# Counting with the mask as the moving operand: four mask tiles at once in quarters of the array

## Chip, cores and metric

The kernel runs on one core of one Trainium2 chip. The metric is the device time of one execution in microseconds (us); the profile shows one execution, with the busy time of each engine: PE (TensorE matmul), PEld (TensorE weight load, beside PE), DVE (VectorE), ACT (ScalarE), POOL (GpSimd) and SP (SyncE, which only issues DMAs here).

## The reference, cut to what matters

Four graph layers work on `x` (2708 x 512) with one dense adjacency matrix `adj` (2708 x 2708, float32, entries not negative, most of them zero). The change touches only the first:

```python
mask = incidence_m > 0
head = mask.astype(incidence_m.dtype)
head = head / jnp.maximum(jnp.sqrt(jnp.sum(head * head, axis=-1, keepdims=True)), EPS)
inc = incidence_m + head
edge_fea = inc @ cur
edge_degree = jnp.sum(inc, axis=-1, keepdims=True)
return edge_fea / edge_degree
```

So before a row of the matrix can be used, its positive entries must be counted: each positive entry is raised by one over the square root of the count of its row. The result goes through a residual and a layer norm, and layers 1 to 3 follow (sums over neighbours with gates and attention, three hops, a normalised convolution).

## The kernel before

The matrix lies transposed in memory (`adjT`: rows are neighbours, columns are the nodes whose sums are made). Nodes and neighbours are cut in two halves of 1354; a half has ten tiles of 128 and one of 74. A **sweep** passes once over the matrix for one layer. It goes through four **ranges** of columns, `RANGES0 = [(768, 256), (0, 384), (384, 384), (1024, 330)]` for the first sweep, each number pair a start and a width within a half. The first range is done plainly: eight products, ten steps each of 256 columns (line 469). The other ranges use a Strassen-like scheme with seven products (line 460: `accu`, `accc`, `accd`, `acca` are its PSUM accumulators; `T1` to `T4` are sums of feature tiles, `a` and `s` tiles of the matrix or sums of them made by DVE on line 405). A step is one tile of 128 neighbours for two column blocks of features; each float32 matmul shows as two passes in the trace, so a step is four passes.

Order is written as a list: `at(pos, fn)` puts a piece of work at a position (a product is one unit, a range seven units, the plain range eight), the list is sorted, and a scheduler then places the instructions on the engines, each of which works in order. Tiles come from pools with a fixed number of buffers: `ring` (38 tiles of the matrix and temporaries), `tmp` (17, among them the tiles loaded for counting), `mask` (6, bfloat16), PSUM (8 banks). A tile of a pool can be written only once the earlier user of its buffer is done.

The counts of a range are made while the range before it is in its products (`extra0`). For each half h of the columns and each of the 22 neighbour tiles i:

- `count_load` brings the tile of `adjT` into a `tmp` buffer, called `cl`. SP issues it for the first counted range, POOL for the later ones. The 74-row tiles need two DMAs.
- `count_mask` makes the mask by two ACT activations, Sign and Relu (lines 714 and 715).
- `count_tile` multiplies with ones: the mask is the stationary operand, 128 columns of it at a time, and a column of ones moves, so three matmuls of one column per tile add up to `cnt`, a PSUM tile with the counts of 128 nodes in each of three columns (line 725).

After the last tile `count_row` makes one over the square root of the count, with a refinement step (DVE, ACT and DVE again on `r`, lines 737 to 745), and `spread_row` lays it out along the free axis: three PE transposes into `pr` (line 753), an ACT copy to `row` (line 756). Then `prep0` (lines 771 and 772, DVE) raises the matrix tiles of the range. The first range's own counts come from the matrix tiles that it has loaded anyway; the same functions serve it.

The list puts the load of tile i 0.7 units ahead of its count, and the mask 0.35 units ahead. The 22 counts of a half are spread over 2.1 to 2.5 units. ACT also copies accumulators out (lines 514 and 531) and applies layer norms (line 567, waiting for DVE's line 564, which waits for the power on POOL, line 562). `run_sums` (lines 774 to 785) makes the row sums for `edge_degree` by matmuls with a column of ones, `rs`; `ds` on line 988 is the like in the second sweep.

The second sweep has a form that the change uses too (`gates` and `gate_tile`, lines 1008 to 1022): four matmuls with 32 stationary columns each, writing partitions 0, 32, 64 and 96 on of one PSUM bank `pg`, an ACT copy to `zg`, and a matmul with `pick` that adds the four partitions. `pick` has ones at rows 0, 32, 64 and 96 of its first column and at rows 1, 33, 65 and 97 of its second.

Of the kernel before, what the change touches and what calls it, by code (L numbers as in the profile page):

```python
# [25 lines left out]
P = 128  # L26
# [32 lines left out]
def wt(k):  # L59
    return min(P, NH - k * P) if k < KT else P  # L60
# [8 lines left out]
def gnn_kernel(ctx: ExitStack, tc: tile.TileContext, x, adjT, w_sa, a_sa, w_gcn, b_gcn, wab, bab, w_hop, w_out,  # L69
               b_out, out):  # L70
    nc = tc.nc
    N, D = x.shape
    NT = 2 * KT
# [13 lines left out]
    ones_bf = const.tile([P, P], BF, name="ones_bf")  # L87
# [27 lines left out]
    pick = const.tile([P, 2], F32, name="pick")  # L115
# [45 lines left out]
    def trans(nm):  # L161
        return pool.tile([P, 384], F32, name=nm, tag="ring", bufs=RING)
# [7 lines left out]
    def bank(nm, shape=None):  # L170
        return psum.tile(shape or [P, D], F32, name=nm, tag="x", bufs=8)
# [6 lines left out]
    def at(pos, fn, hold=False):  # L178

        def go():  # L180
            n = len(nc.cur_bb.bb.instructions)
            fn()
            held.update(range(n, len(nc.cur_bb.bb.instructions)))

        events.append((pos, len(events), go if hold else fn))
# [503 lines left out]
    cnt = {}  # L689
    V = {}  # L690

    def tiles_of(R0, n):
        return list(range(R0 // P, (R0 + n + P - 1) // P))

    def count_load(R0, n, h, i):
        w = wt(i % KT)
        t = tmp("cl")
        j0 = (i // KT) * NH + (i % KT) * P

        move(nc.sync if R0 == RANGES0[1][0] else nc.gpsimd, t[:w, :n], adjT[j0 : j0 + w, h * NH + R0 : h * NH + R0 + n])  # L700
        cnt[R0, h, i] = t

    def count_rows(R0, i):

        return {KT - 1: KA, NT - 1: 32}.get(i, P) if R0 == RANGES0[0][0] else wt(i % KT)

    def count_mask(R0, n, h, i, t=None, on_vector=False):
        w = count_rows(R0, i)
        t = cnt.pop((R0, h, i)) if t is None else t
        cnt[R0, h, i] = m = mask_tile()  # L710
        if on_vector:
            nc.vector.tensor_scalar(m[:w, :n], t[:w, :n], 0.0, None, ALU.is_gt)
        else:
            nc.scalar.activation(m[:w, :n], t[:w, :n], AF.Sign)
            nc.scalar.activation(m[:w, :n], m[:w, :n], AF.Relu)

    def count_tile(R0, n, h, i):

        w = count_rows(R0, i)
        m = cnt.pop((R0, h, i))  # L720
        if i == 0:
            cnt[h] = bank("cnt", [P, 4])
        for j, q in enumerate(tiles_of(R0, n)):
            wq = wt(q)
            nc.tensor.matmul(cnt[h][:wq, j : j + 1], m[:w, q * P - R0 : q * P - R0 + wq], ones_bf[:w, 0:1],
                             start=i == 0 and j == 0, stop=i == NT - 1, skip_group_check=True)

    def count_row(R0, n, h):


        ts = tiles_of(R0, n)
        r = small.tile([P, 4, 4], F32, name="r", bufs=2)
        ps = cnt.pop(h)
        if wt(ts[-1]) < P:
            nc.vector.memset(r[:, 0, :], 1.0)
        for j, q in enumerate(ts):
            nc.vector.tensor_scalar(r[: wt(q), 0, j : j + 1], ps[: wt(q), j : j + 1], 1.0, None, ALU.max)
        m = len(ts)

        c, y, q, t = (r[:, i, :m] for i in range(4))  # L740
        nc.scalar.activation(q, c, AF.Sqrt)
        nc.vector.reciprocal(q, q)
        nc.vector.tensor_tensor(t, q, q, ALU.mult)
        nc.vector.scalar_tensor_tensor(t, c, -0.5, t, ALU.mult, ALU.mult)
        nc.vector.scalar_tensor_tensor(y, t, 1.5, q, ALU.add, ALU.mult)
        cnt[R0, h] = r

    def spread_row(R0, n, h):
        r = cnt.pop((R0, h))
        pr = bank("pr")  # L750
        for j, q in enumerate(tiles_of(R0, n)):
            w = wt(q)
            nc.tensor.transpose(pr[:, q * P - R0 : q * P - R0 + w], r[:w, 1, j : j + 1].to_broadcast([w, P]),
                                ident[:w, :w])
        row[R0, h] = tmp("row")
        nc.scalar.copy(row[R0, h][:, :n], pr[:, :n])  # L756

    def add_run(R0, h, n, w, t):
        if (R0, h) not in run:
            run[R0, h] = tmp("run")  # L760
            if (R0, 1) in run and h == 0:

                nc.vector.tensor_tensor(run[R0, 0][:, :n], run[R0, 1][:, :n], t[:, :n], ALU.add)
                return
            nc.vector.tensor_copy(run[R0, h][:, :n], t[:, :n])
        else:
            nc.vector.tensor_tensor(run[R0, h][:w, :n], run[R0, h][:w, :n], t[:w, :n], ALU.add)
# [6 lines left out]
    def run_sums(R0, n, h, after):  # L774

        ps = bank("rs", [P, 4])
        t = run.pop((R0, h))
        ts = list(range(R0 // P, (R0 + n + P - 1) // P))
        for i, k in enumerate(ts):
            nc.tensor.matmul(ps[: wt(k), i : i + 1], t[:, k * P - R0 : k * P - R0 + wt(k)], ones_f, start=True,  # L780
                             stop=True)
        r = small.tile([P, 4], F32, name="rd", bufs=4)
        for i, k in enumerate(ts):
            after(r[: wt(k), i : i + 1], ps[: wt(k), i : i + 1], h * KT + k, wt(k))
            rd[h * KT + k] = r[:, i : i + 1]

    def extra0(pb, r, R0, n, A):
        if r == 0:
            for h, p, d in ((0, -3.7, 0.05), (1, 1.9, 0.055)):
                for j, i in enumerate([*range(KW), *range(KT, KT + KW), KT - 1, NT - 1]):  # L790
                    key = (f"{h + 1}{i // KT + 1}", i % KT) if i % KT < KW else ("r" if i < KT else "r32", h)
                    a = lambda key=key: A[(0,) + key]
                    at(pb + p + d * (j - 2 * h), lambda h=h, i=i, a=a: count_mask(R0, n, h, i, a(), h == 0 or i % KT == KT - 1))
                    at(pb + p + d * j, lambda h=h, i=i: count_tile(R0, n, h, i))
                    at(pb + (1.7 if h == 0 else 4.8) + 0.06 * j,
                       lambda h=h, i=i, a=a: add_run(R0, h, n, count_rows(R0, i), a()))
                at(pb + p + d * 22, lambda h=h: count_row(R0, n, h))
                at(pb + p + d * 22 + 0.1 * h, lambda h=h: spread_row(R0, n, h))
        if r + 1 < len(RANGES0):
            R1, n1 = RANGES0[r + 1]  # L800
            for h, p, d in ((0, 1.0, 2.5), (1, 3.8, 2.5)) if r else ((0, 3.2, 2.2), (1, 5.4, 2.1)):
                for i in range(NT):
                    q = pb + p + d * i / NT
                    at(q - 0.7, lambda i=i, h=h: count_load(R1, n1, h, i))
                    at(q - 0.35, lambda i=i, h=h: count_mask(R1, n1, h, i))
                    at(q, lambda i=i, h=h: count_tile(R1, n1, h, i))
                at(pb + p + d, lambda h=h: count_row(R1, n1, h))
                at(pb + p + d + 0.15, lambda h=h: spread_row(R1, n1, h))

        def inverse(o, s, t, w):  # L810
            nc.vector.reciprocal(o, s)

        at(pb + (5.2 if r else 3.3), lambda: run_sums(R0, n, 0, inverse))
        at(pb + (4.7 if r else 6.4), lambda: run_sums(R0, n, 1, inverse))
# [43 lines left out]
    for k in range(KW):  # L858
# [6 lines left out]
        at(7.5 + f, lambda k=k: x_last(k))  # L865
    at(9.3, start0)
    sweep(S[0], RANGES0, prep=prep0, extra=extra0, done=done0, first=True, sums=True)


# [79 lines left out]
    i = 0  # L949
# [624 lines left out]
    for n, i in enumerate(list(nc.cur_bb.bb.instructions)):  # L1574
        p = last if n < 3 * strict else done if n in held else {}
# [44 lines left out]
```

## Time and profile before

| | |
|---|---|
| three runs | 2884.59, 2882.81 and 2885.3 us, median 2884.59 |
| span of the profiled execution | 2884.5 us; no time around it is given apart |
| PE busy | 2836.5 us, 98% of the span |
| DVE busy | 2270.4 us, 79% |
| ACT busy | 569.2 us, 20% of the span, nearly all within the first 340 us when masks are made |
| POOL busy | 618.6 us, 21% |
| count matmuls, line 725 | 484, of 0.163 us each (median) |
| mask activations, lines 714 and 715 | 152 each; 0.507 us each (median) for 384 columns |

Busy is the time in which an engine has an instruction under way. Matmuls are pipelined, so the time between two starts, not the length of one, is what an instruction takes from PE. PEclk is the clock that was granted to PE, as a share of the full one. In a list of waits the engine on the left stood idle until the one on the right was done.

### The profile page before, as it was taken

What the parts mean: (1) busy time and instruction counts of PE and PEld (TensorE: products, weight loads), DVE (VectorE), ACT (ScalarE), POOL (GpSimd) and SP (SyncE); (2) the same over time, 40 slices, a digit from 0 to 9 for tenths busy, and PEclk for the clock granted to TensorE, in tenths of its full rate; (3) what the DMA queues carried; (4) which work ended last, traced back from release to release, by engine and by line L of the source; (5) the groups of instructions that cost most, each with busy time, mean ns of one, the idle gap of its engine ahead of it and who ended that gap; (6) DMA issues with size and microseconds to landing.
All of it is one profiled execution on the core that took longest, in us unless ns stands there. A gap on an engine that the chain in (4) does not pass through costs nothing. (4 is left out here: it accounts for less than half of the span.)

```text
span 2884.5 us, 37727 instructions
## 1 busy us (share of the span) xinstructions
PE 2836.5 (98%) x10963; PEld 1870.9 (65%) x10963; DVE 2270.4 (79%) x5879; ACT 569.2 (20%) x1122; POOL 618.6 (21%) x1119
## 2 busy tenths in 40 slices
PE   7999999999999999999999999999999999999998
PEld 6655665657765656866666666666666666666665
DVE  6998698576748675775699787887878878799987
ACT  4554200111146554542100000000000100100001
POOL 0223223123420101132203133031330211501202
PEclk9999999999999999999999999999999999999999
DMA  7666466354544333565668767566675666764542
GB/s 232 201 200 187 131 205 213 123 178 143 183 142 136 117 118 99 154 193 162 193 205 237 212 192 245 172 198 205 189 249 169 181 197 182 225 174 145 176 142 91
DMA packets 373455, 511.52 MB, mean 177 GB/s; under 512 B 63722, under 2 KB 326628, under 8 KB 373248
## 3 DMA queue, kind: packets, MB, share of 16 engines
q1 hardware_dynamic: 307128, 372.01, 44.1%
q0 software_dynamic: 49536, 126.39, 12.7%
q10 hardware_dynamic: 16584, 10.71, 1.3%
q8 instruction: 87, 1.43, 0.2%
q14 instruction: 120, 0.98, 0.1%
HBM read 425.22 MB, written 83.67 MB: 176 GB/s over the span
## 5 line engine op out<-in xcount | busy, mean ns | idle before, releaser
L1231 DVE TENSOR_TENSOR z<-z 128x339 f32<-128x339 f32 (+1 forms) x966 | 453.9, 502 | 13.0 <-PE accu L1286 4.0
L1304 ACT COPY q<-accu 128x338 f32<-128x338 f32 (+1 forms) x84 | 34.6, 443 | 1002.0 <-PE accu L1286 1000.2
L562 POOL TENSOR_TENSOR rstd<-rstd,neg_half 128x1 f32<-128x1 f32 (+3 forms) x91 | 58.4, 642 | 763.9 <-DVE rstd L561 516.3
L1286 PE MATMUL accc<-s,t 128*128 128x338 f32 (+1 forms) x644 | 198.2, 450 | 0.0
L1286 PE MATMUL accu<-z,t 128*128 128x338 f32 (+1 forms) x644 | 194.0, 448 | 1.6 <-DVE z L1231 1.6
L1286 PE MATMUL accd<-z,t 128*128 128x338 f32 (+1 forms) x644 | 193.9, 448 | 0.6 <-DVE q L1368 0.6
L1286 PE MATMUL accc<-z,t 128*128 128x338 f32 (+1 forms) x644 | 193.5, 448 | 0.5 <-ACT q L1304 0.5
L1419 POOL DMA_DIRECT2D Y<-y x192 | 104.9, 553 | 363.0 <-DVE y L1414 331.7
L405 DVE TENSOR_TENSOR a<-a,a 128x384 f32<-128x384 f32 (+2 forms) x330 | 161.2, 509 | 11.5 <-PE accu L460 10.7
L1286 PEld LDWEIGHTS accc<-s,t 128*128 128x128 f32 x644 | 120.9, 190 | 64.1 <-issue 7.5
L1286 PEld LDWEIGHTS accc<-z,t 128*128 128x128 f32 x644 | 122.0, 190 | 61.6 <-issue 1.0
L1286 PEld LDWEIGHTS accu<-z,t 128*128 128x128 f32 x644 | 121.7, 190 | 61.9 <-DVE z L1231 2.1
L1286 PEld LDWEIGHTS accd<-z,t 128*128 128x128 f32 x644 | 121.9, 190 | 60.5 <-DVE q L1368 1.5
L1231 DVE TENSOR_TENSOR s<-z 128x338 f32<-128x338 f32 (+1 forms) x322 | 149.5, 502 | 12.4 <-PE accc L1286 8.4
L1310 DVE TENSOR_TENSOR q<-q,accd 128x338 f32<-128x338 f32 (+1 forms) x112 | 55.9, 499 | 115.0 <-PE accd L1286 115.0
L1083 ACT ACTIVATE e<-row,neg_s 128x384 f32<-128x384 f32 (+5 forms) x176 | 100.5, 571 | 78.2 <-DVE e L1085 18.3
L1085 DVE TENSOR_TENSOR e<-e,f 128x384 f32<-128x384 f32 (+5 forms) x176 | 87.0, 505 | 22.6 <-ACT f L1084 21.5
L1084 ACT ACTIVATE f<-row,neg_s 128x384 f32<-128x384 f32 (+5 forms) x176 | 100.0, 568 | 18.7 <-DVE a L1086 4.5
L974 DVE SCALAR_TENSOR_TENSOR deg<-a,deg 128x384 f32<-128x384 f32 (+2 forms) x152 | 75.1, 504 | 19.8 <-DMA a<-in_adjT 18.7
L1086 DVE SCALAR_TENSOR_TENSOR a<-a,e 128x384 f32<-128x384 f32 (+2 forms) x160 | 79.7, 506 | 5.4 <-DMA a<-in_adjT 3.5
L408 POOL DMA_DIRECT2D As<-a x120 | 64.8, 543 | 83.5 <-DVE a L405 79.7
L771 DVE SCALAR_TENSOR_TENSOR s<-a,row 128x384 f32<-128x384 f32 (+2 forms) x152 | 75.2, 507 | 6.0 <-ACT row L756 6.0
(692 smaller groups left out, 5961.5 us busy)
## 6 DMA issues: line engine op xcount, KB each, us to landing
z<-As SPq DMA_DIRECT2D x320, 169.5 KB
z<-As SPq DMA_DIRECT2D x320, 169.0 KB
a<-in_adjT SPq DMA_DIRECT2D x240, 192.0 KB
z<-in_adjT SPq DMA_DIRECT2D x240, 169.5 KB
z<-in_adjT SPq DMA_DIRECT2D x240, 169.0 KB
a<-in_adjT SPq DMA_DIRECT2D x120, 165.0 KB
a<-in_adjT SPq DMA_DIRECT2D x112, 128.0 KB
As<-a POOLq DMA_DIRECT2D x60, 192.0 KB, 4.3
```

What stands on the lines that cost most here:

```text
L405: nc.vector.tensor_tensor(A[r, dst, k][:, :n], A[r, a, k][:, :n], A[r, b, k][:, :n], op)
L408: nc.gpsimd.dma_start(out=SD[m][k * P : (k + 1) * P, R0 : R0 + n], in_=A[r, dst, k][:, :n])
L562: nc.gpsimd.tensor_tensor(rstd[:w, 1:2], rstd[:w, 0:1], neg_half[:w], ALU.pow)
L771: nc.vector.scalar_tensor_tensor(t[:w, :n], a[:w, :n], 0.0, row[R0, h][:w, :n], ALU.is_gt, ALU.mult)
L974: nc.vector.scalar_tensor_tensor(d[:w, :n], a[:w, :n], 0.0, d[:w, :n], ALU.not_equal, ALU.add)
L1083: nc.scalar.activation(e[:w, :n], row[R0, h][0][:w, :n], AF.Exp, bias=neg_s[:w, t : t + 1])
L1084: nc.scalar.activation(f[:w, :n], row[R0, h][1][:w, :n], AF.Exp, bias=neg_s01[:w, t : t + 1])
L1085: nc.vector.tensor_tensor(e[:w, :n], e[:w, :n], f[:w, :n], ALU.min)
L1086: nc.vector.scalar_tensor_tensor(a[:w, :n], a[:w, :n], 0.0, e[:w, :n], ALU.not_equal, ALU.mult)
L1231: nc.vector.tensor_tensor(d[:, :n], Z[x + (k,)][:, :n], Z[y + (k,)][:, :n], op)
L1286: nc.tensor.matmul(B[home][:, :n], stat(v, k), a[:, :n], start=bool(start and k == 0), stop=k == nk - 1, skip_group_check=True)
L1419: nc.gpsimd.dma_start(out=rows[:, :, f * P : (f + 1) * P], in_=o[32 * f : 32 * (f + 1), : m * P].rearrange("p (b d) -> p b d", d=P))
```

## The change

For the three later ranges the mask becomes the moving operand. `count_four` runs for every fourth tile (and the last): it multiplies the four masks collected so far with 32 columns of ones each, the g-th into partitions 32g to 32g + 31 of one PSUM bank, so that each uses another quarter of the array's columns. The five full groups and one of two add up in the same bank, now 384 columns wide. `count_sums` then copies the bank to a ring tile `zc` on ACT and adds one partition from each quarter by three matmuls with the first column of `pick`, into another bank, `cs`, which `count_row` reads as it read `cnt`. The counts of the first range stay as they were.

```diff
+    def count_four(R0, n, h, i):
+
+        if i % 4 < 3 and i < NT - 1:
+            return
+        i0 = i - i % 4
+        if i0 == 0:
+            cnt[h] = bank("cnt", [P, 384])
+        for g in range(i - i0 + 1):
+            w = count_rows(R0, i0 + g)
+            m = cnt.pop((R0, h, i0 + g))
+            nc.tensor.matmul(cnt[h][32 * g : 32 * g + 32, :n], ones_bf[:w, :32], m[:w, :n], start=i0 == 0,
+                             stop=i0 + g + 4 >= NT, skip_group_check=True)
+
+    def count_sums(R0, n, h):
+
+        z = trans("zc")
+        nc.scalar.copy(z[:, :n], cnt[h][:, :n])
+        cnt[h] = ps = bank("cs", [P, 4])
+        for j, q in enumerate(tiles_of(R0, n)):
+            wq = wt(q)
+            nc.tensor.matmul(ps[:wq, j : j + 1], z[:, q * P - R0 : q * P - R0 + wq], pick[:, 0:1], start=j == 0, stop=True,
+                             skip_group_check=True)
 
     def count_row(R0, n, h):
 
@@
                     at(q - 0.7, lambda i=i, h=h: count_load(R1, n1, h, i))
                     at(q - 0.35, lambda i=i, h=h: count_mask(R1, n1, h, i))
-                    at(q, lambda i=i, h=h: count_tile(R1, n1, h, i))
+                    at(q, lambda i=i, h=h: count_four(R1, n1, h, i))
+                at(pb + p + d, lambda h=h: count_sums(R1, n1, h))
                 at(pb + p + d, lambda h=h: count_row(R1, n1, h))
                 at(pb + p + d + 0.15, lambda h=h: spread_row(R1, n1, h))
```

## The prediction

> **What bounds the kernel now.** I read first the busy time by stretch (columns: stretch, PE, PEld, DVE, ACT, POOL busy us with instruction counts, granted clock, DMA share, GB/s). The counts of the later ranges run between 55 and 330 us.
>
> ```profile
> 0.00:60.00 60.00, 43.58 (x247) 34.48 (x248) 36.56 (x119) 22.17 (x58) 0.70 (x6) 1.00 0.78 232
> 60.00:120.00 60.00, 56.18 (x350) 44.16 (x349) 51.34 (x149) 39.78 (x89) 6.23 (x11) 0.94 0.69 215
> 120.00:230.00 110.00, 109.75 (x490) 64.55 (x489) 96.46 (x244) 53.30 (x117) 32.42 (x58) 1.00 0.62 193
> 230.00:340.00 110.00, 110.00 (x489) 65.04 (x488) 87.88 (x214) 43.50 (x92) 29.91 (x53) 1.00 0.53 157
> ```
>
> From 120 to 340 us PE is the bound: time on it is time of the kernel, as far as DVE (80 to 88% busy) keeps up. From 60 to 120 us PE, ACT and DVE are all near their limit and the clock was granted at 0.94. Next, PE in order of time (start, length, engine, line):
>
> ```profile
> 150.20 1.54 PE L460 MATMUL accd<-a,T1A 128*128 128x384 f32 x4
> 151.57 0.22 PE L725 MATMUL cnt<-ones_bf,mask 74*128 74x1 bf16 x3
> 151.65 1.54 PE L460 MATMUL accd<-a,T1A 128*128 128x384 f32 x4
> 153.03 0.22 PE L725 MATMUL cnt<-ones_bf,mask 128*128 128x1 bf16 x3
> ...
> 158.83 0.59 PE L725 MATMUL cnt<-ones_bf,mask 128*128 128x1 bf16 x18
> 159.29 0.89 PE L460 MATMUL accc<-a,T4A 128*128 128x384 f32 x2
> ...
> 161.30 2.74 PE L460 MATMUL accd<-a,T1D 128*128 128x384 f32 x8
> 163.88 1.45 PE L460 MATMUL accu<-a,T2A 128*128 128x384 f32 x4
> ```
>
> Eight plain f32 passes take 163.88 - 161.30 = 2.58 us, 0.3225 each. Four passes and one count tile (three one-column matmuls) repeat every 153.03 - 151.57 = 1.46 us; less 4 x 0.3225 = 1.29, **a count tile costs PE 0.16 us**. Last, who waits for whom, 36 to 120 us for PEld and 0 to 340 us for ACT and POOL (total us, times, longest):
>
> ```profile
> PEld L725 <- ACT mask L715: 4.1, 6, 2.4
> PEld pr L753 <- DVE r L745: 2.5, 2, 2.2
> ACT mask L714 <- PE cnt L725: 33.6, 35, 4.1
> POOL cl L151 <- ACT mask L714: 70.2, 30, 18.1
> ```
>
> In the first counted range PE waits for masks; later ACT is up to six masks ahead and waits for a mask buffer (35 times), which only a count releases. So the ring of six is full and is what protects PE.
>
> **What the Trainium skill says.** "TensorEngine Tiling (Array Packing)", Key Properties: different tiles of the array load weights and multiply in parallel, and changing the tiling mode drains the engine. The second sweep already has this shape in f32 (gate sums, line 1012), and agrees:
>
> ```profile
> 514.92 0.81 PE L460 MATMUL accd<-a,B22B 128*128 128x384 f32 x2
> 515.66 0.52 PE L1012 MATMUL pg<-C,wab_pad 128*32 128x384 f32 x2
> 515.67 0.52 PE L1012 MATMUL pg<-W,wab_pad 128*32 128x384 f32 x2
> 516.01 0.49 PE L1012 MATMUL pg<-C,wab_pad 128*32 128x384 f32 x2
> 516.02 0.49 PE L1012 MATMUL pg<-W,wab_pad 128*32 128x384 f32 x2
> 516.45 1.56 PE L460 MATMUL accd<-a,B22B 128*128 128x384 f32 x4
> ```
>
> The quarters start about 10 ns apart. From 514.92 the two passes before should end at 515.565; the group holds PE from there to 516.45 = 0.885 us, and the first pass after it starts its successor about 0.10 late (the four passes take 1.40 instead of 1.29 us in the same pattern at 547.75): 0.98 in all, 0.34 more than its two streaming passes of 0.3225. That 0.34 is the drain into and out of quarter mode. "TensorE: Matmul & The Clock Gate", section "Wait — 56ns, not 53.3ns?", prices a warm matmul at N / 2.4 GHz + 2.5 ns: an estimated 0.16 us for 384 bf16 columns and 0.14 for 330. No run here shows a wide bf16 matmul; the f32 pass at 0.3225 is twice that, which fits. The same page, "What's actually happening", says that an idle window of about 3.4 us halves the clock for the next; the 0.94 above is two such windows, each costing 3.4 / 2 = 1.7 us.
>
> **The change, part by part.** (1) Removed: 3 ranges x 2 halves x 22 tiles = 132 count tiles. The 88 of 384 columns at 0.162 are 14.3, less 0.4 because six of them stand together (0.54 for 18 matmuls instead of 0.97); the 44 of 330 columns at 0.173 (same subtraction at 245 to 278 us) are 7.6. Sum **-21.5**. (2) Added: per range and half five groups of four and one of two, 36 in all. A group costs 0.34 + 0.16 = 0.50 (24 of them, 12.0) or 0.34 + 0.14 = 0.48 (12, 5.8): **+17.8**. A group of two pays the same. Bounds: 0.33 if half of the drain belongs to f32 weights, 0.66 if the stream runs at the f32 rate. (3) Added: the sums, six times three f32 matmuls of one column with 128-column weights. The like is line 988 (ds, six passes): 0.67 with 384, about 0.58 with 330 columns around it, so 4 x 0.67 + 2 x 0.58 = **+3.8**. The work on PE comes to **+0.1**: the saving of 0.65 - 0.50 per four tiles is eaten by the half groups and the sums.
>
> (4) Waits. The copy zc on ACT (0.46 us, like zg) and the wait of cs for it come between the last count and r. In the first counted half the built order puts zc behind four masks of the next half. In the trace before, these end at 88.6, PE's last count is at 87.6 and pr at 90.7. Then zc is done near 89.2, PE reaches cs about 88.4 and waits 1; cs takes 0.67, and the 2.7 us from counts to pr follow: pr about 2 later. While PE waits at cs, all matmuls queue; while r heads DVE's queue, the run sums behind it wait, and the copy row and the masks on ACT. Of this about 1 comes back, since four masks then lie ready and PE's small waits for masks at 91 and 93 go. I take **+1.0** (from -3, if the six us of waits and one slow-clock window go, to +4). In the other halves cs stands one to three steps behind the last group and pr some three steps behind cs; a step is 1.29, the chain is 2.7 to 4, so little shows: **+0.3** (0 to 3). In the last half pr stands one step later in PE's order than before; its row then reaches DVE 1.3 later, and DVE is packed until PE waits for it at 369 us (1.4 + 0.4 + 0.4 of gaps at T1C): **+1.0** (0 to 2.5).
>
> (5) Masks: four are held until the fourth is there, and two buffers remain. The last two of a group cannot start before the group before has run: 2 x 2 x 0.507 = 2.0 us of ACT against about four steps of PE, 3.45 in the range with 256 columns, 5.2 later. That fits unless ACT is held by a layer-norm or accumulator copy. Loads follow masks: POOL's cl loads (88 full, 8 rests) wait on masks already, the pow of the norm stands behind them, and SP's 44 and 4 likewise. I take nothing, because 1.4 to 3 us of slack cover 0.7 us ACT copies; uncovered, see the slow rival. (6) One more PSUM bank and one ring slot, six times for a few us: nothing, since PE shows no wait for an adjacency load from 120 to 340 us; one late load would cost up to its 4 us landing.
>
> Sum: 2884.5 + 0.1 + 1.0 + 0.3 + 1.0 = 2886.9. The profiled span is 0.1 below the median 2884.59, so that is the forecast: **2887**. A measurement of this kernel can tell 0.2% (5.8 us) from no change.
>
> **Rivals.** *Slower, by the mask ring.* Instead of up to six finished masks PE has at most two of the next group ahead. In the first counted range (twelve groups, 58 to 118 us) ACT needs 4 x 0.97 = 3.9 us for four masks and PE 3.45 + 0.50 between groups: no slack to make good an ACT wait for a norm (2.9 and 2.1 us at 75 and 81). If each group finds its last mask 0.9 late, that is 11 us, and such pauses bring one or two more half-clock windows, 1.7 to 3.4: 2897 to 2900. It decides from 0.5 us a group. For it: the 4.1 us that PE waits already. Against it: from 120 us on ACT waits for PE, not PE for ACT. *Faster, by cheap quarters.* At 0.33 a group (2) falls by 6; with one slow-clock window and some of the six us of waits gone, 2884.5 + 0.1 - 6 - 2 = 2877. Against it: the drain is the same mode change as in pg. *Not parallel.* If bf16 quarters ran one after another, a group would be 0.34 + 0.64 = 0.98: +17, 2904. The starts 10 ns apart speak against it.
>
> **Numbers.** A wash within 5.8 us 0.53; mask ring and longer count chains 0.32; not parallel 0.03; cheap quarters 0.12. The wash alone spans 2881 to 2890. From 2879 to 2899 leaves out the fast rival's core and the serial case with the worst of the ring, about 2 in 10. Faster 0.12, same 0.53, slower 0.35.
>
> **What would show it.** Quarter matmuls starting within 20 ns of each other and 0.50 us of PE per group; cs and its neighbours 0.6 to 0.7; pr of the first half near 93 us; more waits of PE on DVE at T1C of the last range; no PE wait for masks after 120 us. I am wrong if a group costs under 0.40 or over 0.60, if PE waits for masks add over 5 us, or if the clock from 60 to 120 us falls below 0.9 or rises to 1.0.

## Result, and the profile after

The changed kernel takes **2891.18 us** (median of 9 runs, 2883.38 to 2893.94) against 2883.92 (9 runs, 2880.51 to 2886.63) of the kernel before beside it: a ratio of 1.0023, 95% interval 1.0014 to 1.0031. Two more sets on other occasions gave 1.0019 (1.0011 to 1.0026) and 1.0018 (1.0011 to 1.0024). So it is slower by 5 to 7 us, at the bound of what was called no change. The profiled execution took 2888.01 us with a span of 2886.2; 1.8 us lie around the span, and this execution was one of the quicker ones.

First the busy time by stretch of the changed kernel, with the columns as in the prediction:

```profile
0.00:60.00 60.00, 42.76 (x243) 33.82 (x244) 36.85 (x121) 22.61 (x58) 0.70 (x6) 1.00 0.79 234
60.00:120.00 60.00, 56.03 (x284) 42.12 (x283) 52.74 (x157) 41.24 (x93) 6.25 (x11) 0.97 0.65 206
120.00:230.00 110.00, 109.68 (x409) 62.42 (x408) 93.45 (x229) 51.72 (x117) 32.09 (x58) 1.00 0.62 198
230.00:340.00 110.00, 109.77 (x414) 62.89 (x413) 89.02 (x218) 39.14 (x94) 29.26 (x53) 1.00 0.51 155
```

The count of PE instructions falls (490 to 409 from 120 to 230 us), the busy time does not: PE is still full. From 60 to 120 us this execution had one half-clock window (a stretch in which PE was granted half the clock), the kernel before two. ACT, at 39.8 of 60 us, was not near its limit there before, unlike PE and DVE; and 159 of its 569 busy us lie before 340 us (22.2 + 39.8 + 53.3 + 43.5), not nearly all.

Next, PE in order of time:

```profile
150.93 0.35 PE L738 MATMUL cnt<-mask,ones_bf 128*32 128x384 bf16 x4
151.20 2.85 PE L460 MATMUL accd<-a,T1B 128*128 128x384 f32 x8
153.98 0.35 PE L738 MATMUL cnt<-mask,ones_bf 128*32 128x384 bf16 x4
154.26 0.91 PE L460 MATMUL accc<-a,T4A 128*128 128x384 f32 x2
```

From 151.20 to 154.26 stand eight f32 passes, 8 x 0.3225 = 2.58, and one group: 3.06 - 2.58 = 0.48. Taken so over all groups of four that can be measured like this, the median is 0.474 us with 384 columns and 0.451 with 330; a group of two takes 0.467 and 0.444. The four quarters start 3 to 4 ns apart. Last, the chain of the first counted half, in order of time (in brackets: idle before it, and who ended it), and PE's waits from 36 to 120 us:

```profile
88.43 0.83 PE L748 MATMUL cs<-pick,zc 128*128 128x1 f32 x6 [1.17 <-ACT zc L744]
89.12 1.11 PE L469 MATMUL accc<-aw,B21C 128*128 128x256 f32 x4
90.68 0.54 PE L776 MATMUL pr<-ident,r 128*128 128x128 f32 x3 [0.45 <-DVE r L768]
```

```profile
PE cnt L738 <- ACT mask L715: 2.4, 1, 2.4
PE pr L776 <- DVE r L768: 1.5, 2, 1.1
PE cnt L725 <- ACT mask L715: 1.2, 4, 0.3
PE cs L748 <- ACT zc L744: 1.2, 1, 1.2
```

The new wait at cs is there, pr comes at 90.7 as before, and one group waits 2.4 us for its fourth mask. Waits for masks are 2.4 + 1.2 = 3.6 us in all; before, the like was

```profile
PE cnt L725 <- ACT mask L715: 3.2, 5, 2.0
```

From 120 to 340 us PE waits for no mask.

Where the time goes is read from the start of one and the same PE matmul in two profiles. The table gives it less its start in the profile of the kernel before, in us. The tags in the first column stand for the runs of the next section.

| kernel | 50 us | 340 us | 560 us | 2800 us | half-clock windows up to 600 us, at |
|---|---|---|---|---|---|
| before | 0 | 0 | 0 | 0 | 84, 91, 436 |
| changed | -1.1 | -0.9 | 0.8 | 1.7 | 82, 437, 594 |
| changed, e1 | 0.3 | 0.5 | 2.1 | 2.9 | 84, 436 and 439 |
| changed, e9 | -1.4 | 1.7 | 2.6 | 0.3 | 88 and 91, 436 and 439 |
| e2, order of before | 0.1 | 2.0 | 2.4 | 4.2 | 85, 92, 436 |
| e3, before in other order | -0.2 | -0.7 | 0.5 | 1.1 | 83, 435 |
| e4, first range only | -0.8 | 1.1 | 0.7 | 1.4 | 88 and 92, 437 |
| e5, last row earlier | 0.2 | 1.6 | -1.6 | 1.7 | 84, 593 |

A window is 3.413 us long and costs up to half of that, 1.7. Between 50 and 340 us the changed kernel is 0.2, 0.2 and 3.1 us slower than before in three profiles, but the first two had one half-clock window in this stretch and before had two. Up to 120 us, where the windows lie, profiles can be compared with the same number of them. With two windows the change since 50 us is 0.0 in e6 and e7, which count the first range as before, and +1.3 to +2.5 in e2, e4 and e9, which count it in groups. With one it is -1.0 in e3, which counts as before, and -1.0 to 0.0 in five profiles with groups (changed, e1, e5, e11, e12). So groups in the first range cost 0 to 2.5 us, and the missing window hid part of that. Between 340 and 560 us, after the last count, the changed kernel loses 0.9 to 1.7 in all three.

From 502 us on the instructions and their order are the same on every engine of the kernel before and the changed one, yet between 560 and 2800 us the profiles of the table gain up to 2.3 or lose up to 3.3 us against that of before (a window at 593 or 594 is in two of them), so totals are compared by medians.

### The profile page after: what moved, and what is told of

The parts are those of the page before. It is cut to its first block, busy times and chain, and to the rows that moved or that the text cites. A ratio compares the mean times of both kernels' runs of the same rounds, so it can differ in the third digit from the quotient of the medians.

```text
span 2886.2 us, 37290 instructions
## 1 busy us (share of the span) xinstructions
PE 2835.7 (98%) x10735; PEld 1864.2 (65%) x10735; DVE 2270.3 (79%) x5879; ACT 565.2 (20%) x1128; POOL 618.7 (21%) x1119
## 5 line engine op out<-in xcount | busy, mean ns | idle before, releaser
L608 PE MATMUL ps_d<-w,xT 128*128 128x512 f32 (+1 forms) x176 | 79.2, 592 | 0.0
```

Of the source, the lines that this page charges most:

```text
L608: nc.tensor.matmul(o, lhs(c), r, start=c == 0 and n == 0, stop=c == DC - 1, skip_group_check=True)
```

## Experiments

**e1 and e9: the changed kernel again.**

> The changed kernel once more, to see whether its 7 us (ratio 1.0023) come back and where a second profile puts them. Counting theory (the cost lies between 36 and 345 us, in groups, sums and their waits): ratio 1.0023, and PE is behind before by 5 us or more at 345 us. Order theory (the build has written another DVE order from 330 to 600 us, and the loss comes there): ratio 1.0023, PE within 2 us of before at 345 us and 3 or more behind at 600 us.

> The changed kernel a third time, beside its variants on one chip. If its loss is a property of the kernel: 1.0012 to 1.0028, and a mean granted clock below that of the kernel before by 0.0005 or more. If it was chance in which executions fell on a half-clock window: 1.0000 to 1.0010.

Measured: 2892.43 against 2887.17 us (1.0019) and 2888.61 against 2883.63 (1.0018). The loss belongs to the kernel. Over all executions of a set the mean granted clock was 0.9971 against 0.9978 in e1 and 0.9972 against 0.9981 in e9. 0.0007 to 0.0009 of 2885 us is 2.2 to 2.5 us, or 1.3 to 1.4 windows more in an execution: **about half of the loss goes with a slower clock**. By the scatter of the executions (95%) each figure is good to about 1.2 us. Where the extra windows lie no set of single profiles can say; doubled windows at 436 us are seen in both of these profiles and not in the one of the kernel before. At 345 us PE was 0.5 behind and at 600 2.0, which is nearer to the order theory than to the counting theory, though it falls short of the 3 that this theory asked for; in e9 PE was already 1.7 behind at 340.

**e2 and e3: the order of DVE exchanged.** With the change the scheduler wrote another order for DVE, in the traces until 501 us, and with it for PE (117 to 389 us) and POOL (419 to 497 us). In e2 the changed kernel's DVE was bound to the order of before from the last count row on; in e3 the DVE of the kernel before was bound to the order of the changed one. PE and POOL were left to the scheduler, and PE's order from 369 to 388 us is in neither run quite that of the kernel whose DVE order was taken.

```diff
+    ORDER = {mybir.EngineType.DVE: [696, 698, 697, ...]}
+    for e, order in ORDER.items():
+        own = [i for i in nc.cur_bb.bb.instructions if i.engine == e]
...
+        for k, m in zip(order, order[1:]):
+            tc.add_manual_dep(own[m], own[k].name, ...)
```

> The changed kernel with one thing forced: from the last count row on (330 us) DVE takes its instructions in the order of the kernel before; counting is as in the changed kernel. Order theory: the loss is gone, 0.9990 to 1.0008 (2881 to 2886 us). Counting theory: nothing comes back, 1.0015 to 1.0030.

> The kernel before, counting as before, but from the last count row on DVE takes its instructions in the order of the changed kernel. Order theory: slower by what the change cost, 1.0014 to 1.0030 (2888 to 2893 us). Counting theory: no change, 0.9993 to 1.0007.

Measured: e2 1.0014 (1.0007 to 1.0020), e3 1.0002 (0.9993 to 1.0010). The theory as stated falls: the order alone costs nothing that shows in the total (at most 2.9 us by the interval), and taking it away leaves 3.8 of the 5.3 us that e1 shows in the same set. And e2 has nearly the clock of before, 0.9976 against 0.9978: slow windows are not what it loses. The step itself can be seen. First the end of DVE's work for the products of the last range in the kernel before, then in the changed kernel (PE's `ps_n` can start only when `P1c` is there):

```profile
432.21 0.54 DVE L405 TENSOR_TENSOR a<-a,a 128x384 f32<-128x384 f32 x1
432.68 0.41 DVE L227 TENSOR_TENSOR T2C<-B22C,T1C 128x256 f32<-128x256 f32 x1
433.02 0.41 DVE L229 TENSOR_TENSOR T3C<-B22C,T3C 128x256 f32<-128x256 f32 x1
433.35 0.54 DVE L405 TENSOR_TENSOR s<-a,a 128x384 f32<-128x384 f32 x1
433.82 0.89 DVE L521 TENSOR_TENSOR P1c<-P1c,acca 128x330 f32<-128x330 f32 x2
```

```profile
432.80 0.55 DVE L405 TENSOR_TENSOR s<-a,a 128x384 f32<-128x384 f32 x1
433.26 0.41 DVE L227 TENSOR_TENSOR T2C<-B22C,T1C 128x256 f32<-128x256 f32 x1
433.60 0.41 DVE L229 TENSOR_TENSOR T3C<-B22C,T3C 128x256 f32<-128x256 f32 x1
433.94 0.55 DVE L998 SCALAR_TENSOR_TENSOR deg<-a,deg 128x384 f32<-128x384 f32 x1
434.40 0.55 DVE L405 TENSOR_TENSOR a<-a,a 128x384 f32<-128x384 f32 x1
434.87 0.90 DVE L521 TENSOR_TENSOR P1c<-P1c,acca 128x330 f32<-128x330 f32 x2
```

One more instruction of the next sweep, `deg`, stands ahead of `P1c`: 0.46 us. DVE is also 0.6 us later than in the kernel before at this place, while PE is 0.6 earlier. Together, 434.87 - 433.82 + 0.62 = 1.67 us, which is what PE's wait grew by, from 2.1 to 3.8. The waits of PE from 340 to 640 us, one line each of the kernel before, the changed kernel, e2 and e3:

```profile
PE ps_n L591 <- DVE P1c L521: 2.1, 1, 2.1
```

```profile
PE ps_n L591 <- DVE P1c L521: 3.8, 1, 3.8
```

```profile
PE ps_n L591 <- DVE P1c L521: 2.5, 1, 2.5
```

```profile
PE ps_n L591 <- DVE P1c L521: 3.6, 1, 3.6
```

The wait follows the order in every run: 3.2 to 3.9 us in the nine profiles with the changed kernel's kind of order there, 2.1 to 2.6 in the five with that of before, 1.3 us apart by their means. From 340 to 560 us e3 and e6 (below), which count as before, lose 1.2 and 1.6 us like the changed kernel, so what is lost there goes with the order. But their totals show no loss that can be told from zero, so this cannot be the 5.

**e4, e7 and e8: one range at a time.**

```diff
-                    at(q, lambda i=i, h=h: count_four(R1, n1, h, i))
-                at(pb + p + d, lambda h=h: count_sums(R1, n1, h))
+                    at(q, lambda i=i, h=h: (count_four if r == 0 else count_tile)(R1, n1, h, i))
+                if r == 0:
+                    at(pb + p + d, lambda h=h: count_sums(R1, n1, h))
```

(e4; `r == 1` in e7, `r == 2` in e8.)

> Groups of four and sums in the first counted range only (58 to 118 us); the two later ranges count as before, and the order of DVE from the later ranges on is that of the kernel before. Order theory: no loss, 0.9990 to 1.0007. Mask ring or count chain in the first counted range as the cause: 1.0015 to 1.0030. A cost in every range alike: a third of it, 1.0008.

> Groups and sums in the second counted range only (120 to 220 us), the others count as before. Late-row theory: no loss, 0.9992 to 1.0006, since the last row is where it was. Counting theory: about half of the loss, 1.0008 to 1.0014.

> Groups and sums in the last counted range only (230 to 340 us), the others count as before. Late-row theory: the whole loss, 1.0014 to 1.0026. Counting theory: about half of it, 1.0008 to 1.0014.

Measured: 0.9995 (0.9987 to 1.0004), 1.0002 (0.9994 to 1.0011) and 1.0001 (0.9992 to 1.0009). No range by itself costs anything that can be told from zero (at most 3.2 us by the widest interval). The 2.2 us that e4's profile loses between 50 and 120 us do not show in its total either (at most 1.2 us). The three add up to 0.9998, give or take 0.0015, and the whole is 1.0018 to 1.0023. The mean clock of the three, 0.9976, 0.9981 and 0.9978, is within 0.0002 of that of before. e8 has groups and sums in the last range, its late row and the changed kernel's order of DVE behind it (PE waits 3.4 us for `P1c`), so these three together do not cost 5 us either.

**e5 and e6: the last row alone.** In the changed kernel the steps from the counts to the last row stand later, so e5 takes them forward, and e6 puts them back in the kernel before. e5 does this by spreading the last half's counts over 2.3 units instead of 2.5, which brings the row forward beyond its place in the kernel before: it is copied at 331.7 us, against 332.6 before and 333.1 in the changed kernel.

```diff
-            for h, p, d in ((0, 1.0, 2.5), (1, 3.8, 2.5)) if r else ((0, 3.2, 2.2), (1, 5.4, 2.1)):
+            for h, p, d in ((0, 1.0, 2.5), (1, 3.8, 2.3 if r == 2 else 2.5)) if r else ((0, 3.2, 2.2), (1, 5.4, 2.1)):
```

```diff
-                at(pb + p + d, lambda h=h: count_row(R1, n1, h))
-                at(pb + p + d + 0.15, lambda h=h: spread_row(R1, n1, h))
+                late = 0.1 if (r, h) == (2, 1) else 0
+                at(pb + p + d + late, lambda h=h: count_row(R1, n1, h))
+                at(pb + p + d + 0.15 + late, lambda h=h: spread_row(R1, n1, h))
```

> The changed kernel, with the counts of the last half spread over 2.3 units instead of 2.5: its row (cs, the steps on r, pr) stands six PE passes earlier than in the changed kernel and four earlier than in the kernel before; groups and sums as in the changed kernel. Late-row theory (the loss comes from this one row, which finds DVE full and leaves it behind up to 440 us): the loss is gone, 0.9990 to 1.0007. Counting theory (groups and sums of the two later ranges cost in every execution): it stays, 1.0012 to 1.0025.

> The kernel before, counting as before, but the row of the last half (steps on r and pr) put 0.1 units later in the list, so that pr stands two passes later in PE's order, where the changed kernel has it; the order of DVE from there on is that of the changed kernel too. Late-row theory: slower by 1.0010 to 1.0022. Counting theory: no change, 0.9994 to 1.0006.

Measured: e5 1.0006 (0.9998 to 1.0014), e6 1.0000 (0.9992 to 1.0008). With the row earlier, about two thirds of the loss is gone by the medians, though groups and sums are all there; the intervals of e5 and of the changed kernel overlap, though, and they come from different sets. In e5's profile PE waits for `P1c` 2.6 us, and its three waits at T1C near 370 us (1.8 us together in the kernel before) are gone. The kernel before with its row as early as in e5 was not run, so how much of e5's gain any kernel would have from this is open.

e6 shows where the new order comes from: with nothing but the late row, PE, DVE and POOL have the changed kernel's order from 333 us on in its trace. So late row and new order of all engines together cost nothing that shows. That groups and sums cost only together with them is possible, but e8 speaks against it for the last range.

**e10, e11 and e12: the price of a group, and the ring of masks.** e10 counts each tile alone against 128 columns of ones, without quarters:

```diff
...
-        for g in range(i - i0 + 1):
-            w = count_rows(R0, i0 + g)
-            m = cnt.pop((R0, h, i0 + g))
-            nc.tensor.matmul(cnt[h][32 * g : 32 * g + 32, :n], ones_bf[:w, :32], m[:w, :n], start=i0 == 0,
-                             stop=i0 + g + 4 >= NT, skip_group_check=True)
+        w = count_rows(R0, i)
+        m = cnt.pop((R0, h, i))
+        nc.tensor.matmul(cnt[h][:, :n], ones_bf[:w], m[:w, :n], start=i == 0, stop=i == NT - 1, skip_group_check=True)
...
```

e11 has eight mask buffers (`RING = 37`, mask `bufs=8`). e12 is e11 with six masks to a group in the later ranges (`i % 6`, and `c = 32 * ((i0 + g) % 4)` for the quarter).

> The mask moves as in the changed kernel, but each tile is counted alone, when its mask is there, against 128 columns of ones; no quarters and no holding of four masks; zc and the sums stay, with one partition taken. If the drain and the pass are priced right, a tile takes 0.16 us of PE and shows no drain: 132 x 0.16 = 21.1 us instead of 16.8, so +4.3 us on the changed kernel (+0.0015), and the wait for the fourth mask near 82 us is gone. If holding four masks is what costs, this one is no slower than the changed kernel, or faster.

> The changed kernel with eight mask buffers instead of six, for which the ring has 37 tiles instead of 38 (that alone alters the planned order all over the kernel, by an amount that only this run shows). Mask-ring theory: PE's waits for masks from 36 to 120 us shrink from 3.6 us to under 1.5, and PE reaches 345 us at least 2 us earlier than in the changed kernel. Otherwise: those waits stay, and PE at 345 us is within 1 us of the changed kernel.

> As the run with eight mask buffers, but in the two later ranges six masks are counted at once (six matmuls in four quarters), so that a half drains PE four times instead of six. If a group costs 0.315 us for the drain and 0.16 for each layer of four: three groups of 0.63 and one of 0.475 instead of six of 0.475, 0.46 less in a half of 384 columns; over four halves about 2 us less than the run with eight buffers by 345 us (0.9993 of it). If the drain is hidden by other work: no difference.

e10: 1.0025 (1.0017 to 1.0033), 2891.74 us beside 2888.61 of e9, **+3.1**. Its PE in order of time:

```profile
142.87 0.33 PE L734 MATMUL cnt<-mask,ones_bf 128*128 128x384 bf16 x1
143.03 1.45 PE L460 MATMUL accc<-s,T3C 128*128 128x384 f32 x4
144.32 0.33 PE L734 MATMUL cnt<-mask,ones_bf 128*128 128x384 bf16 x1
```

144.32 - 142.87 = 1.45 for four passes (1.29) and one mask: 0.16, and 0.140 by the median with 330 columns. Nothing is paid beside the pass. A group of four without its pass of 0.16 is thus 0.474 - 0.163 = 0.311 us for the change into quarters and back. What it is made of the runs do not separate: 0.10 of it is the first f32 pass after the group, and the first pass after the sums `cs`, which use the whole array, is 0.08 late too (0.406 us to the next instead of 0.323). The work is 88 x 0.163 + 44 x 0.140 = 20.5 us instead of 16.8, +3.7; the +3.1 fits. A wait of 2.0 us for a mask is there too (2.4 in the changed kernel), so it does not come from holding four.

e11: 1.0045 (1.0032 to 1.0058). PE's waits from 36 to 120 us:

```profile
PE cnt L738 <- ACT mask L715: 2.4, 1, 2.4
...
PE cnt L725 <- ACT mask L715: 1.4, 5, 0.3
```

Two more buffers change nothing in them, and PE is 1.7 us behind the kernel before at 340 us, as in e9. **The mask ring is not the cause** of PE's waits for masks. In its profile 9 us more come after 600 us, where the ring of 37 has brought another order of DVE (up to 2645 us), and over its five executions the mean clock is 0.9960, against 0.9981 of the kernel before: some 6 of its 13.7 us. Buffers, ring and order changed together here, so which of them costs this is open.

e12: 1.0035 (1.0022 to 1.0047), 2.1 us below e11 by the medians (5 and 6 runs, whose intervals overlap) and 4.0 us earlier in the profiles at 340 us, 2.6 of it between 120 and 340 us, where the two differ. Its PE:

```profile
141.09 2.85 PE L460 MATMUL accc<-s,T3C 128*128 128x384 f32 x8
143.77 2.74 PE L460 MATMUL accc<-s,T3D 128*128 128x384 f32 x8
146.35 4.03 PE L460 MATMUL accd<-a,T1A 128*128 128x384 f32 x12
150.32 0.50 PE L740 MATMUL cnt<-mask,ones_bf 128*32 128x384 bf16 x6
150.75 2.85 PE L460 MATMUL accd<-a,T1B 128*128 128x384 f32 x8
```

28 passes are 9.03 us; 150.75 - 141.09 - 9.03 = 0.63 for six masks: the change of mode once, the pass twice. The price of a group is thereby confirmed; the 2 us that it saves fit the totals, but five and six executions are too few to show them.

None of these kernels beats the kernel before by more than the measurement can tell; e4 comes nearest.

## Why the prediction was right or wrong

The time lies in the range, 4 us above the likeliest value, and on the border between "same" and "slower". The price of the work was understood; that the total still fell within a range of 20 us owes something to the width of the range, for the slowdown, 5.0 to 7.3 us, is two to three times the forecast +2.4. None of the signs named for being wrong came: a group cost 0.47, PE waited 3.6 us for masks, and the clock from 60 to 120 us was 0.97. Point by point:

- **(1), (2), (3), the work on PE: right.** Groups took 0.474 and 0.451 us for a forecast 0.50 and 0.48, so 36 of them 16.8 us instead of 17.8. The sums took 0.670 and 0.580, as forecast. With the 21.5 removed PE has 0.9 less to do, not 0.1 more. That changing the tiling mode drains the engine is what "TensorEngine Tiling (Array Packing)", Key Properties, in the Trainium skill says; e10, which changes no mode, pays no such 0.31 us, and half groups pay all of it (0.467 of 0.474).
- **(4), the first half: right in its kind.** PE waited 1.2 us at cs (forecast 1) in the profile, 2.6 in that of e9; pr came at 90.7, not near 93, since the chain behind cs took 90.68 - 89.12 = 1.6 us and not 2.7. The cost, 0 to 2.5 us with the windows made equal, lies around the forecast 1.0.
- **(4), the other halves: not contradicted.** From 120 to 340 us three profiles of the changed kernel give +0.5 to +0.6 against before (forecast 0.3 of waits, and the work), but e3 and e6, which count as before, give +0.6 and -0.4.
- **(4), the last half: the wrong place.** The row is copied at 333.1 us, 0.5 later than before while PE was 0.9 earlier: 1.4, forecast 1.3. But PE's waits on DVE there are 1.6 us as against 1.8, for PE's own order was rewritten as well. First before, then changed:

```profile
369.40 1.38 PE L460 MATMUL accd<-a,T1C 128*128 128x330 f32 x4 [1.24 <-DVE a L405]
371.05 1.38 PE L460 MATMUL accd<-a,T1C 128*128 128x330 f32 x4 [0.27 <-DVE a L405]
```

```profile
368.49 1.27 PE L460 MATMUL accc<-a,T4A 128*128 128x330 f32 x4
370.57 1.38 PE L460 MATMUL accd<-a,T1C 128*128 128x330 f32 x4 [0.81 <-DVE a L405]
371.79 0.72 PE L460 MATMUL accc<-a,T4A 128*128 128x330 f32 x2
```

Passes on T4A, which were ready, now stand between those on T1C. The wait that grew is the one at P1c at 432 us, by 1.7, and e3 has it without a late row: it goes with the order. So the term was near its size and had the wrong path.
- **(5) and the slow rival: it was right to take nothing.** Waits for masks are 3.6 us against 3.2 before. Eight buffers left the 2.4 us wait as it was, and counting each mask at once left 2.0 of it.
- **(6): right.** No wait for an adjacency load appeared.
- **What failed is the sum, +2.4.** The term that it lacks is the half-clock windows: the likeliest value adds none (the slow rival named one or two more, from pauses for masks, which did not come); over the executions there are 1.3 to 1.4 more, 2.2 to 2.5 us. It also did not see that the order of DVE, PE and POOL behind the change would be rewritten until 501 us; what that is worth, some 1.3 us at P1c, happens to be near the 1.0 that was set down for the last half.

**What stays open.** The whole costs 5 us, while each range alone, the late row alone and the order alone cost nothing that could be told from zero; their intervals leave room for 1 to 3 us each. A lower mean clock is seen only with all ranges together, and it is gone when the last row stands earlier (0.9977 in e5) or DVE keeps the old order (0.9976 in e2). Yet e2 is still 3.8 us slower, and where it loses them was not found. Why a window is slow in one execution and not in the next was not tested: one profile of each set does not show where the extra windows of the others lie.

## What to carry to other kernels

Before small matmuls are packed into quarters between full ones, price the mode change: here 0.31 us a time, as much as two of the passes of 0.16, so that four masks came out at 0.47 instead of 0.65 and, with half groups and sums, gained 0.9 us of PE work in all. Packing more masks behind one change costs less for each (six at 0.63), though no total here shows a gain from it. Where a scheduler plans the order, a small shift in the list (here one row, in e6) can rewrite the order of several engines long after it; compare the built orders up to the end, and look for what now stands ahead of the next stage's first input.

## What the hardware showed that was not expected

- A bf16 mask of 384 columns that moves against 128 columns of ones takes 0.163 us of PE, as long as the same mask held stationary for three one-column matmuls (0.162). With 330 columns it is 0.140 against 0.173. Moving the mask, without quarters, is already no dearer, the sums apart.
- A group of two quarters costs 0.467 us and one of four 0.474: a quarter more costs 3 to 4 ns.
- Two half-clock windows may follow each other without a break, 6.83 us at half clock (at 436 us in e1 and e9), behind a PE wait of 3.9 and 3.6 us. It is no rule: in the changed kernel's first profile one window followed a wait of 3.8 us at the same place.
